# First 21 products of the output projection between the last unit's head pairs, its other operands in the space of queries and keys, the last weight sums in the units

## The chip, the cores and the metric

The kernel runs on one core of one Trainium2 chip. The metric is device microseconds (us) from launch to end. Engines: TensorE (PE, with its weight loads PEld), VectorE (DVE), ScalarE (ACT), GpSimd (POOL), and SyncE (SP), which here issues all DMAs, one after the other: an issue that must wait for a semaphore holds back all issues behind it.

## The reference

All of it is fp32, on x of shape (8, 512, 1024): eight batch elements of 512 rows.

```python
def _L0_attn_ref(h, Wq, Wk, Wv, Wo):            # 16 heads of 64
    q, k, v = h @ Wq, h @ Wk, h @ Wv            # split into heads; rotary embedding on q and k
    logits = where(causal, q @ k.T, -1e9) / sqrt(64)
    return (softmax(logits) @ v) @ Wo

def _L0_ffn_ref(x, weight, bias, lora_A, lora_B, starts):
    y = x @ weight.T + bias
    return y + (x @ A.T) @ Bw.T                 # one of 3 adapters of rank 16 per batch element, or none

x = x + layernorm(attn(layernorm(x), Wq, Wk, Wv, Wo))
x = x + layernorm(ffn(layernorm(x), weight, bias, lora_A, lora_B, starts))
```

## The kernel before

**Products.** Every large matrix product of a batch element (512 x 1024 by 1024 x 1024) is done by the Strassen-Winograd scheme twice over: 7 x 7 = 49 small products instead of 64, at the price of sums of operands and of results. The outer level has seven groups, P1 to P7 (`GROUPS`): P1 is L11·R11, P2 is L12·R21, P4 is L22·T4, P5 is S1·T1, P7 is S3·T3, P6 is S2·T2, P3 is S4·R22, done in that order (`ORDER`). L and S are the weight's blocks and their sums, R and T those of the activations. S1 to S4 and the inner sums of the weights are made once ("weight sums") and kept in DRAM; T1 to T4 are made on the spot by `sum_right`, each from R blocks and the T before: T1 = R12 − R11, T2 = R22 − T1, T4 = R21 − T2, T3 = R22 − R12. Each outer group is seven small products of two matmuls (128x128 weights, 128x256 moving), collected in PSUM accumulators acca to accd, and drained by `drain`: DVE additions into p1 and u2, ACT copies, and results A, U, c11, c12, c21, c22. `combine` adds these to each other on DVE or POOL.

**Ticks.** The order of everything is written out by hand. The list `events` maps a tick, one small product, to the calls that are issued with it (`at(tick, fn)`), and `run(tick, filler)` issues first the events marked "pe", then the product itself, then the rest. All engines and SP take their instructions in that order.

**Stages.**
- The V projection, with the first layer norm, 8 x 49 ticks (until about 432 us).
- Eight units of Q and K projections (`plan_unit`, `unit_product`), 49 ticks each. A unit is a half of the heads for two batch elements. The results (A, B, D, E, F) are added and rotated on DVE and POOL and moved by DMA to the tiles qk. In units 1 to 7 the eight head pairs of the unit before stand between the products (class `Pair`: `scores` s, `exps`, `scale`, `transpose` ptp, `keep` pT, `values` po, `store` ops, `sum` opt). Operands come by DMA through a ring, `load_slot`, eight products ahead.
- The last unit's eight pairs alone ("the tail"), where no unit products are left: `Pair(u, n).plan(base + 51 + 6 * n, alone=True)`. In a pair, scores of the first two query blocks, of the third (s_2) and of the fourth (s_3) come one after another. The fourth block's scores of this unit lie in two of the three accumulator banks `ps_p`, the others in the one buffer `ps_s`. When a batch element's last pair is stored, four POOL sums (`sum`, opt) complete the operand, which SP stores to attn in DRAM. The tile opt has one buffer.
- The output projection of batch elements q = 0 to 7 and the FFN (q = 8 to 15), by `products`, 49 ticks each, with the layer norms, residuals, transposes and the adapters' first product (`lora_in`, ph) of the element before between them.

**Weight sums.** `plan_part` makes one of 24 chunks (8 for the second half of Q and K, 8 for Wo, 8 for the FFN weight): a load of 512 KB, eight sums on POOL, a store of 1568 KB, in one buffer. Units 1 to 7 do three each, the tail does three.

**Memory.** The tail frees the ring and its neighbours (`streams`) and puts the Wo blocks L11, L12, L22, S1 (pool `wop`) and the right operands of q = 0 (pool `gp`) there. S3, S2, S4 (pool `wop2`) and everything that the projection needs otherwise lie in the space of the attention's pools (`phase_a`), so they can only be opened when the attention is through.

**Right operands of the next element.** `plan_right` loads R11, R21, R12, R22 of q + 1 at ticks 10, 17, 24, 31 of q into the tiles that the earlier operands leave (`next_roles`), and makes T1, T2, T4, T3 at 38, 45, 52, 63, on POOL while q + 1 is an output projection.

Of the kernel before, what the change touches and what calls it, by code (L numbers as in the profile page):

```python
# [17 lines left out]
P = 128  # L18
# [114 lines left out]
def sandwich_kernel(  # L133
# [60 lines left out]
    def at(tick, fn, kind=None):  # L194
        events[tick].append((kind, fn) if kind else fn)
# [42 lines left out]

    def load_sums(pool, name, n, tag):

        t = LW[name][n] = pool.tile([P, 8, 7, 64], F32, tag=tag, name=f"{name}_{n}")
        nc.sync.dma_start(out=t, in_=w2_d[name][:, :, 7 * SLOT_L[n] : 7 * SLOT_L[n] + 7])

# [40 lines left out]
    def open_c(q, tag):  # L284
        C[q, tag] = env["cp"].tile(
            [P, 2, HALF], F32, tag=tag, bufs=env["cbufs"] if tag[0] == "c" else 1, name=f"{tag}_{q}"
        )

    class Group:
# [42 lines left out]
        def drain(self, p):  # L332

            acc, t = self.acc, self.t
            add = lambda out, x, a: nc.vector.tensor_tensor(out, acc[a], x, op=ALU.add)  # L335
            if p == "P1":
                for n, k in (("p1", 1), ("u2", 2)):
                    t[n] = env["tmp"].tile([P, SUB], F32, tag=n, bufs=k, name=f"{n}_{self.name}")
# [22 lines left out]

    def products(q0, count, order):


        cur, before, todo = None, None, None

        def fill(q, g, p):
            nonlocal cur, before, todo
            if p == 0:
                before = cur  # L370
                cur = Group(q, order(q)[g]) if q < q0 + count else None
            name = SLOTS[p]
            group = before if name == "P3" else cur
            if group:
                group.product(name)
            if todo:
                todo[0].drain(todo[1])
            todo = (group, name) if group else None

        for n in range(count * N2 + 4):  # L380
            q, m = divmod(n, N2)
            g, p = divmod(m, NP)
            run(n, lambda q=q, g=g, p=p: fill(q0 + q, g, p))
# [26 lines left out]
    def norm(key, dst, src):  # L410
# [8 lines left out]
    env.update(  # L419
        cbufs=1, small=right(stay, "small0", 4), cp=right(stay, "cp0"), tmp=right(stay, "tmp0")  # L420
    )
    gvp, wvp, wvl = (right(operands, name) for name in ("gv", "wv", "wvl"))
    ps_p = env["acc"] = psum.enter_context(tc.tile_pool(name="ps_p0", bufs=1, space=PSUM))
# [169 lines left out]
    PAIRS = B  # L593
    phase_a, streams, work2 = ExitStack(), ExitStack(), {}

# [119 lines left out]
    class Pair:  # L715
# [14 lines left out]
        def scores(self, qbs):  # L730
            qT, kT = (qk[self.u, self.i][:, :, self.s, w] for w in range(2))
            if self.u + 1 == UQ and qbs[0] == 3:
                ps = [
                    ps_p.tile([P, S], F32, tag="acc", name=f"s_{self.name}_{qbs[0]}_{j}") for j in range(2)
                ]
            else:
                ps = ps_s.tile([P, 2, S], F32, tag="s", name=f"s_{self.name}_{qbs[0]}")
                ps = [ps[:, j, :] for j in range(2)]
            at = 0
            for qb in qbs:  # L740
                L = (qb + 1) * P
                for j in range(2):
                    r = slice(j * HD, (j + 1) * HD)
                    nc.tensor.matmul(  # L744
                        ps[j][:, at : at + L],
                        lhsT=qT[r, qb],
                        rhs=kT[r, : qb + 1],
                        start=True,
                        stop=True,
                    )  # L750
                self.ps[qb] = [p[:, at : at + L] for p in ps]
                at += L

        def exps(self, qbs):
            pr = work2["work"].tile([P, 2, S], F32, tag="pr", bufs=4, name=f"pr_{self.name}_{qbs[0]}")
            at = 0
            for qb in qbs:
# [5 lines left out]
                for j in range(2):  # L763

                    nc.vector.tensor_tensor_reduce(  # L765
                        out=v[:, j, :],
                        in0=self.ps[qb][j],
                        in1=work2["mask"][:, S - L :],
# [84 lines left out]
        def plan(self, base, last=12, alone=False):  # L853
# [16 lines left out]
            if self.i == NH - 1:  # L870
                for m, k in enumerate((1, 2, 3, 4, 6)):
                    at(base + last + k, lambda m=m: self.sum(m))
# [67 lines left out]
    cur, before = None, None  # L940

    def unit_product(n):
        nonlocal cur, before
        u, m = divmod(n, N2)
        m, p = divmod(m, NP)
        if p == 0:
            before, cur = cur, quad_group(u, m)
        cur.product(p)
        if p:
            cur.drain(p)  # L950
        elif before:
            before.drain(NP)
        load_slot(n + 8)

    for u in range(UQ + 1):
# [14 lines left out]
        else:  # L970
# [3 lines left out]
            streams.close()  # L974
            wop = tc.alloc_tile_pool(name="w2", bufs=1)
            gp = tc.alloc_tile_pool(name="g2", bufs=1)
            for k, n in ((14, "R11"), (16, "R12"), (18, "R22"), (20, "R21")):
                at(base + k, lambda n=n: load_right(gp, 0, n))
            for k, n in ((24, "L11"), (30, "L12"), (36, "L22"), (42, "S1")):
                at(base + k, lambda n=n: load_sums(wop, "wo", n, n))  # L980
            for k, n in ((26, "T1"), (30, "T2"), (34, "T4"), (38, "T3")):
                for m in range(3):
                    at(base + k + m, lambda n=n, m=m: sum_right(gp, 0, n, nc.gpsimd, slice(m, m + 1)))
            run_rest()
    phase_a.close()


    with ExitStack() as a:
        wop2 = a.enter_context(tc.tile_pool(name="w2b", bufs=1, side="right"))
        cp = a.enter_context(tc.tile_pool(name="cp", bufs=1, side="right"))  # L990
        lc = a.enter_context(tc.tile_pool(name="lc", bufs=1, side="right"))
        rows = a.enter_context(tc.tile_pool(name="rows", bufs=3, side="right"))
# [4 lines left out]
        env.update(acc=ps_p, cp=cp, tmp=tmp, small=small, cbufs=2)  # L997
# [6 lines left out]
        lb_sb = lc.tile([P, E], F32, name="lb_sb")  # L1004
        nc.gpsimd.memset(lb_sb, 0.0)
        env["lb"] = lb_sb
        nc.sync.dma_start(out=lb_sb[0:NR, :], in_=lora_b)
        nc.sync.dma_start(out=lb_sb[HD : HD + NR, :], in_=lora_b)
        nc.sync.dma_start(out=lb_sb[NR : NR + 1, :], in_=bias)

# [158 lines left out]

        load_sums(wop2, "wo", "S3", "S3")  # L1170
        for n, k in (("S2", 3), ("S4", 9)):
            at(k, lambda n=n: load_sums(wop2, "wo", n, n))
        for q in range(NQ):
# [10 lines left out]
            for k, e, res, l, r in (  # L1184
# [7 lines left out]
            ):  # L1192
                at(base + k, lambda a=(q, res, l, r, e): combine(*a))
# [6 lines left out]
    gp.release()  # L1200
    wop.release()

# [90 lines left out]
```

## Time and profile before

| | |
|---|---|
| time, median of 3 runs | 2529.23 us (2528.59 to 2531.31) |
| the profiled execution | 2532.83 us, span 2530.8 us |
| mean granted TensorE clock | 0.984 |
| busy time of PE, DVE, POOL, ACT | 2402.4 (95%), 1733.9 (69%), 1500.0 (59%), 1097.2 us (43%) |
| DMA | 606.00 MB, mean 239 GB/s |
| units 2, 3 and 4 | 148.6 us each |
| the tail | the last unit product is issued at 1578 us; the first product of the output projection starts at 1689.69 us |

The profile is that of one execution. Its page has the busy share of each engine by 40 slices of the span; the trace behind it has each instruction with its start, its time and, in brackets, how long its engine was idle before it and which instruction ended that. Neighbouring instructions of one kind are drawn together (x4 is four of them). Tile names are cut of their numbers: `accb_P<-wo_L,R` is a product of an L block of Wo on an R block; `wo_S` is one of the S blocks.

### The profile page before, as it was taken

The page shows a single profiled execution, that of the slowest core. Times are in us where ns is not written, and L with a number is a line of the kernel's source. Part 1 is how long each engine was busy: PE and PEld are TensorE (multiplying, and loading weights), DVE is VectorE, ACT ScalarE, POOL GpSimd, SP SyncE. Part 2 cuts the span into 40 slices and gives each one's busy share as a digit, 9 for nine tenths or more (in the row PEclk, how much of TensorE's full clock was granted, in tenths as well). Part 3 has the DMA queues.
Part 4 walks back from the last instruction along what each step waited for, and adds up shares of the span by engine and source line. Part 5 has one row for each costly group of instructions (what it writes and reads, how often), then busy time and mean ns, then how long its engine had stood idle before and what let it go on. Part 6 is the DMA issues. An engine that isn't in the chain of part 4 may idle for free. (4 is left out here: it accounts for less than half of the span.)

```text
span 2530.8 us, 37109 instructions
## 1 busy us (share of the span) xinstructions
PE 2402.4 (95%) x12192; PEld 1885.9 (75%) x12192; DVE 1733.9 (69%) x3842; ACT 1097.2 (43%) x2748; POOL 1500.0 (59%) x1127
## 2 busy tenths in 40 slices
PE   6999998989999999999999999788999999999997
PEld 4887887777777777777777766357888887888886
DVE  8777676284957668585775858645777777766676
ACT  3323321025555555555555565752444443222222
POOL 4978774225363453626355363365677686887885
PEclk8999999999999999999999999899999999999999
DMA  7687888899899898989788894766656677334434
GB/s 257 209 281 256 256 262 261 283 292 274 255 311 275 263 317 254 324 250 327 250 272 315 234 316 143 242 230 242 212 167 210 220 266 271 126 130 141 142 104 137
DMA packets 415665, 606.00 MB, mean 239 GB/s; under 512 B 127889, under 2 KB 243601, under 8 KB 410866
## 3 DMA queue, kind: packets, MB, share of 16 engines
q1 hardware_dynamic: 415474, 603.64, 73.2%
q8 instruction: 98, 1.61, 0.3%
q14 instruction: 93, 0.76, 0.1%
HBM read 368.65 MB, written 201.33 MB: 225 GB/s over the span
## 5 line engine op out<-in xcount | busy, mean ns | idle before, releaser
L775 ACT ACTIVATE pr<-pr,nm 128x128 f32<-128x128 f32 (+3 forms) x512 | 280.8, 550 | 173.5 <-DVE nm L765 173.5
L786 ACT ACTIVATE pr<-pr,rs 128x128 f32<-128x128 f32 (+3 forms) x512 | 251.8, 551 | 109.8 <-DVE rs L783 109.8
L765 DVE CUSTOM_DVE_ANT_0 pr<-s,mask 128x128 f32<-128x128 f32 (+3 forms) x512 | 224.2, 484 | 36.6 <-PE s L744 34.6
L632 PE MATMUL accb_q_P<-xs,ls 128*128 128x256 f32 x896 | 218.1, 387 | 6.9 <-DVE u_q_P L116 6.9
L632 PE MATMUL accc_q_P<-xs,ls 128*128 128x256 f32 x896 | 218.6, 387 | 5.4 <-DVE E_q L116 5.4
L632 PE MATMUL acca_q_P<-xs,ls 128*128 128x256 f32 x896 | 219.4, 388 | 0.8 <-issue 0.8
L1040 POOL TENSOR_TENSOR c<-c,row 128x512 f32<-128x512 f32 x120 | 160.6, 1359 | 90.5 <-ACT c L412 84.5
L632 PEld LDWEIGHTS accc_q_P<-xs,ls 128*128 128x128 f32 x896 | 166.3, 191 | 53.4 <-issue 23.7
L632 PEld LDWEIGHTS acca_q_P<-xs,ls 128*128 128x128 f32 x896 | 166.7, 191 | 51.9 <-issue 21.6
L632 PEld LDWEIGHTS accb_q_P<-xs,ls 128*128 128x128 f32 x896 | 166.4, 191 | 51.0 <-DMA ls<-wqk 8.1
L744 PE MATMUL s<-qk 64*128 64x128 f32 (+3 forms) x1024 | 192.9, 471 | 4.2 <-DVE nm L765 2.4
L275 POOL TENSOR_TENSOR T<-R,T 128x512 f32<-128x512 f32 (+1 forms) x96 | 174.0, 1839 | 33.3 <-DVE u_P L335 17.4
L800 PE MATMUL ptp<-ident,pr 128*128 128x128 f32 x1280 | 178.4, 278 | 11.4 <-ACT pr L786 6.7
L800 PEld LDWEIGHTS ptp<-ident,pr 128*128 128x128 f32 x1280 | 147.4, 142 | 46.4 <-ACT pr L786 11.4
L673 POOL TENSOR_TENSOR B_q<-B_q,m 128x1024 f32<-128x1024 f32 x16 | 39.7, 2480 | 237.6 <-DVE B_q L671 237.6
L820 PE MATMUL po<-pT,v 128*64 128x384 f32 (+3 forms) x1024 | 158.8, 448 | 20.8 <-ACT pT L814 17.0
L558 POOL TENSOR_TENSOR wc_g<-wc_g 128x256 f32<-128x256 f32 (+1 forms) x120 | 122.9, 1043 | 90.5 <-DMA wc_g<-in_wqk_dram 74.9
L820 PEld LDWEIGHTS po<-pT,v 128*64 128x64 f32 x1024 | 71.1, 139 | 115.5 <-issue 66.9
L335 DVE TENSOR_TENSOR p_P<-accb_P,p_P 128x256 f32<-128x256 f32 x112 | 46.3, 413 | 107.8 <-PE accb_P L313 58.6
L335 DVE TENSOR_TENSOR u_P<-accb_P,p_P 128x256 f32<-128x256 f32 x112 | 47.3, 423 | 98.1 <-ACT p_P L339 98.1
L814 DVE COPY pT<-ptp 128x512 f32<-128x512 f32 (+1 forms) x136 | 82.8, 614 | 43.5 <-PE ptp L800 43.5
L632 PE MATMUL accd_q_P<-xs,ls 128*128 128x256 f32 x448 | 108.9, 386 | 1.1 <-ACT E_q L125 0.7
(1077 smaller groups left out, 5790.3 us busy)
## 6 DMA issues: line engine op xcount, KB each, us to landing
ls<-wqk SPq DMA_DIRECT2D x392, 256.0 KB, 4.4
xs<-xop SPq DMA_DIRECT2D x392, 256.0 KB, 4.7
R<-attn SPq DMA_DIRECT2D x32, 896.0 KB, 5.5
wqk<-wc_g SPq DMA_DIRECT2D x16, 1568.0 KB, 9.4
x<-in_x_dram SPq DMA_DIRECT2D x32, 512.0 KB, 9.5
v<-vd SPq DMA_DIRECT2D x64, 256.0 KB, 5.2
attn<-ops SPq DMA_DIRECT2D x16, 1024.0 KB, 8.4
row<-in_x_dram SPq DMA_DIRECT2D x32, 512.0 KB, 6.1
```

What stands on the lines that cost most here:

```text
L275: eng.tensor_tensor(RX[q, n][:, c], RX[q, x][:, c], RX[q, y][:, c], op=ALU.subtract)
L335: add = lambda out, x, a: nc.vector.tensor_tensor(out, acc[a], x, op=ALU.add)
L558: eng.tensor_tensor(out, x, y, op=op)
L632: nc.tensor.matmul(acc[:, :, w, :], lhsT=ls[:, k, w, :], rhs=xs_[:, :, k, :], start=(first and w == 0 and k == 0), stop=True, skip_group_c ...
L744: nc.tensor.matmul(ps[j][:, at : at + L], lhsT=qT[r, qb], rhs=kT[r, : qb + 1], start=True, stop=True,)
L765: nc.vector.tensor_tensor_reduce(out=v[:, j, :], in0=self.ps[qb][j], in1=work2["mask"][:, S - L :], scale=-1.0 / HD**0.5, scalar=3.0e38, o ...
L775: nc.scalar.activation(v[:, j, :], v[:, j, :], AF.Exp, bias=nm[:, j : j + 1], scale=-1.0, accum_out=sm[:, j : j + 1],)
L786: nc.scalar.mul(v, v, rs[:, j : j + 1])
L800: nc.tensor.transpose(pt[:, n, :], self.pr[qb][:, j, ts(kb, P)], ident)
L814: copy(self.pT[j][:, : qb + 1, ts(qb, P)], self.pt[j][:, : qb + 1, :])
L820: nc.tensor.matmul(po[j * HD : (j + 1) * HD, kb * P :], lhsT=self.v[:, kb, ts(j, HD)], rhs=self.pT[j][:, kb, kb * P :], start=(kb == 0), s ...
L1040: nc.gpsimd.tensor_tensor(c, c, row[q, t][:, ts(h, HALF)], op=ALU.add)
```

## The change

It has these parts.

- The first 21 products of q = 0 (P1, P2, P4, which need L11, L12, L22, R11, R21, T4) are issued in the tail by a new `first_product`, into accumulators of `ps_p`: eight at ticks 20, 23, … 41, two in each of the periods of pairs 2 to 5, and thirteen at ticks 44 to 56. `products` then begins at tick 21 (`AHEAD`). Accordingly the fourth block's scores go back to the single buffer `ps_s`.
- The tail's pools `wop`, `gp` and two small ones (`cl`, `tl`) are opened after the chunk buffer is closed too; loads of R11 and L11 stand at tick 10, R12 15, R22 17, L12 21, R21 24, L22 31, S1 42; T1 at 21, T2 26, T4 32, T3 44.
- `qk` and its neighbour close at tick 49, before the rest of the attention; S3, S2, S4 are loaded into their space at ticks 49, 54, 56.
- Units 4, 5 and 6 do four chunks of weight sums (ticks 4, 13, 22, 31) instead of three (9, 19, 29), the tail none.
- The opt sums of the last two pairs' elements come at +0, 0, 0, 0, 1 ticks behind their store instead of +1, 2, 3, 4, 6.
- For q = 1, R12, R22, R11, R21 are loaded at ticks 21, 29, 30, 33, T1 at 44; c21 += c12 of q = 0 (tick 38) now stands ahead of T1 on POOL.
- The adapters la_sb and lb_sb are cleared (POOL) and loaded at tick 79 instead of ahead of tick 0.

```diff
-    def load_sums(pool, name, n, tag):
+    def load_sums(pool, name, n, tag, queue=nc.sync):
...
+                env["u2"].reverse()
+                for n, pool in (("p1", env["p1"]), ("u2", env["u2"][0])):
+                    t[n] = pool.tile([P, SUB], F32, tag=n, name=f"{n}_{self.name}")
...
-        for n in range(count * N2 + 4):
+        for n in range(first, count * N2 + 4):
...
-            if self.u + 1 == UQ and qbs[0] == 3:
-                ps = [
-                    ps_p.tile([P, S], F32, tag="acc", name=f"s_{self.name}_{qbs[0]}_{j}") for j in range(2)
-                ]
-            else:
-                ps = ps_s.tile([P, 2, S], F32, tag="s", name=f"s_{self.name}_{qbs[0]}")
-                ps = [ps[:, j, :] for j in range(2)]
+            ps = ps_s.tile([P, 2, S], F32, tag="s", name=f"s_{self.name}_{qbs[0]}")
...
-                for m, k in enumerate((1, 2, 3, 4, 6)):
+                for m, k in enumerate((0, 0, 0, 0, 1) if alone else (1, 2, 3, 4, 6)):
...
-        for name, bufs in (("small", 4), ("ops", 2), ("qk", 5), ("v", 3), ("work", 2), ("ac", 1), ("ch", 1)):
-            work2[name] = right(phase_a, name, bufs)
+        for name, bufs in (("small", 4), ("ops", 2), ("v", 3), ("work", 2), ("ac", 1), ("qk", 5), ("ch", 1)):
+            to = {"ac": rows_qk, "qk": rows_qk, "ch": chunks}.get(name, phase_a)
+            work2[name] = right(to, name, bufs)
...
-        for k in () if u == 0 else (9, 19, 29) if u < UQ else (6, 22, 38):
+        for k in () if u in (0, UQ) else (4, 13, 22, 31) if u in (4, 5, 6) else (9, 19, 29):
...
+    AHEAD = 3 * NP
+
+    def first_product(n):
+        nonlocal cur, before
+        m, p = divmod(n, NP)
+        if p == 0:
+            L, R, tag = GROUPS[ORDER[m]]
+
+            def mm(acc, p, first):
+                l, r, _ = PRODUCTS[p]
+                for k in range(2):
+                    nc.tensor.matmul(
+                        acc, lhsT=RX[0, R][:, SLOT_R[r], k, :],
+                        rhs=LW["wo"][L][:, 4 * k : 4 * k + 4, SLOT_L[l], :],
+                        start=(first and k == 0), stop=True, skip_group_check=True,
+                    )
...
+            before, cur = cur, Product(nc, ps_p, tl, [P, SUB], f"0_{ORDER[m]}", mm, dest)
+        cur.product(p)
+        if p:
+            cur.drain(p)
+        elif before:
+            before.drain(NP)
...
-            wop = tc.alloc_tile_pool(name="w2", bufs=1)
-            gp = tc.alloc_tile_pool(name="g2", bufs=1)
-            for k, n in ((14, "R11"), (16, "R12"), (18, "R22"), (20, "R21")):
-                at(base + k, lambda n=n: load_right(gp, 0, n))
-            for k, n in ((24, "L11"), (30, "L12"), (36, "L22"), (42, "S1")):
-                at(base + k, lambda n=n: load_sums(wop, "wo", n, n))
-            for k, n in ((26, "T1"), (30, "T2"), (34, "T4"), (38, "T3")):
+            chunks.close()
+
+            wop, gp, cl = (tc.alloc_tile_pool(name=name, bufs=1) for name in ("w2", "g2", "cl"))
+            env["cl"] = cl
+            tl = tc.alloc_tile_pool(name="tl", bufs=1)
+            for k, n in (
+                (10, "R11"), (10, "L11"), (15, "R12"), (17, "R22"), (21, "L12"), (24, "R21"), (31, "L22"), (42, "S1"),
+            ):
...
+            for k, n in ((21, "T1"), (26, "T2"), (32, "T4"), (44, "T3")):
                 for m in range(3):
                     at(base + k + m, lambda n=n, m=m: sum_right(gp, 0, n, nc.gpsimd, slice(m, m + 1)))
+            at(base + 52, lambda: combine(0, "c11", "c11", "A", nc.vector))
+            cur, ticks = None, [*range(20, 44, 3), *range(44, 57)]
+            for k in range(10, 57):
+                if k in (54, 56):
+                    n = {54: "S2", 56: "S4"}[k]
+                    load_sums(wop2, "wo", n, n)
+                if k == 49:
+                    rows_qk.close()
+                    wop2 = tc.alloc_tile_pool(name="w2b", bufs=1)
+                    load_sums(wop2, "wo", "S3", "S3")
+                if k in ticks:
+                    run(base + k, lambda n=ticks.index(k): first_product(n))
+                else:
+                    run(base + k, None)
+            cur.drain(NP)
...
-        nc.gpsimd.memset(la_sb, 0.0)
-        nc.sync.dma_start(out=la_sb[:, :, 0:NR], in_=lora_a.rearrange("(k p) r -> p k r", p=P))
...
+        def load_adapters():
+            nc.gpsimd.memset(la_sb, 0.0)
...
+        at(N2 + 30, load_adapters)
...
-            at(base + 6, next_roles)
+            at(max(base + 6, AHEAD), next_roles)
             for n, k in (("R11", 10), ("R21", 17), ("R12", 24), ("R22", 31)):
+                if q == 1:
+                    k = AHEAD + {"R12": 0, "R22": 8, "R11": 9, "R21": 12}[n]
...
-            for n, k in (("T1", 38), ("T2", 45), ("T4", 52), ("T3", 63)):
+            for n, k in (("T1", 44 if q == 1 else 38), ("T2", 45), ("T4", 52), ("T3", 63)):
...
-        load_sums(wop2, "wo", "S3", "S3")
-        for n, k in (("S2", 3), ("S4", 9)):
-            at(k, lambda n=n: load_sums(wop2, "wo", n, n))
...
-        products(0, NQ, lambda q: ORDER if q + 1 < NQ else LAST)
+        products(0, NQ, lambda q: ORDER if q + 1 < NQ else LAST, AHEAD)
```

More of the change, by code (lines that the diff above doesn't have):

```diff
@@ L237, in sum_left @@
         eng.tensor_tensor(W[n][:, c], W[x][:, c], W[y][:, c], op=op)
-    def load_sums(pool, name, n, tag):
+    def load_sums(pool, name, n, tag, queue=nc.sync):
         t = LW[name][n] = pool.tile([P, 8, 7, 64], F32, tag=tag, name=f"{name}_{n}")
-        nc.sync.dma_start(out=t, in_=w2_d[name][:, :, 7 * SLOT_L[n] : 7 * SLOT_L[n] + 7])
+        queue.dma_start(out=t, in_=w2_d[name][:, :, 7 * SLOT_L[n] : 7 * SLOT_L[n] + 7])
     def open_right(pool, q, n):
@@ L284, in open_c @@
     def open_c(q, tag):
-        C[q, tag] = env["cp"].tile(
-            [P, 2, HALF], F32, tag=tag, bufs=env["cbufs"] if tag[0] == "c" else 1, name=f"{tag}_{q}"
+        first = q >= 0 and (tag == "A" or tag in ("c11", "c21") and q % 2 == 0)
+        two = q >= 0 and tag in ("c12", "c22")
+        C[q, tag] = env["cl" if first else "cp"].tile(
+            [P, 2, HALF], F32, tag=tag, bufs=1 + two, name=f"{tag}_{q}"
         )
@@ L336, in drain @@
             if p == "P1":
-                for n, k in (("p1", 1), ("u2", 2)):
-                    t[n] = env["tmp"].tile([P, SUB], F32, tag=n, bufs=k, name=f"{n}_{self.name}")
+                env["u2"].reverse()
+                for n, pool in (("p1", env["p1"]), ("u2", env["u2"][0])):
+                    t[n] = pool.tile([P, SUB], F32, tag=n, name=f"{n}_{self.name}")
                 nc.scalar.copy(t["p1"], acc["a"])
@@ L360, in sandwich_kernel, with products @@
     )
-    def products(q0, count, order):
+    def products(q0, count, order, first=0):
         cur, before, todo = None, None, None
@@ L419, in sandwich_kernel @@
     env.update(
-        cbufs=1, small=right(stay, "small0", 4), cp=right(stay, "cp0"), tmp=right(stay, "tmp0")
+        small=right(stay, "small0", 4), cp=right(stay, "cp0"), p1=right(stay, "tmp0")
     )
+    env["u2"] = [env["p1"], right(stay, "tmp1")]
     gvp, wvp, wvl = (right(operands, name) for name in ("gv", "wv", "wvl"))
@@ L593, in sandwich_kernel @@
     PAIRS = B
-    phase_a, streams, work2 = ExitStack(), ExitStack(), {}
+    phase_a, chunks, rows_qk, streams, work2 = *(ExitStack() for _ in range(4)), {}
     def start_ring():
@@ L744, in scores @@
                     nc.tensor.matmul(
-                        ps[j][:, at : at + L],
+                        ps[:, j, at : at + L],
                         lhsT=qT[r, qb],
@@ L750, in scores @@
                     )
-                self.ps[qb] = [p[:, at : at + L] for p in ps]
+                self.ps[qb] = ps[:, :, at : at + L]
                 at += L
@@ L766, in exps @@
                         out=v[:, j, :],
-                        in0=self.ps[qb][j],
+                        in0=self.ps[qb][:, j, :],
                         in1=work2["mask"][:, S - L :],
@@ L939, in sandwich_kernel @@
     assert not todo
-    cur, before = None, None
+    cur = before = tl = None
     def unit_product(n):
@@ L953, in unit_product, with dest @@
         load_slot(n + 8)
+    AHEAD = 3 * NP
[12 more added lines that the diff above has]
+                    )
+            def dest(i, j):
+                if (0, tag) not in C:
+                    open_c(0, tag)
+                return C[0, tag][:, j, ts(i, SUB)]
+            before, cur = cur, Product(nc, ps_p, tl, [P, SUB], f"0_{ORDER[m]}", mm, dest)
[4 more added lines that the diff above has]
+            before.drain(NP)
     for u in range(UQ + 1):
@@ L974, in sandwich_kernel @@
             streams.close()
-            wop = tc.alloc_tile_pool(name="w2", bufs=1)
-            gp = tc.alloc_tile_pool(name="g2", bufs=1)
-            for k, n in ((14, "R11"), (16, "R12"), (18, "R22"), (20, "R21")):
-                at(base + k, lambda n=n: load_right(gp, 0, n))
-            for k, n in ((24, "L11"), (30, "L12"), (36, "L22"), (42, "S1")):
-                at(base + k, lambda n=n: load_sums(wop, "wo", n, n))
-            for k, n in ((26, "T1"), (30, "T2"), (34, "T4"), (38, "T3")):
+            chunks.close()
[5 more added lines that the diff above has]
+            ):
+                if n in ("R11", "R12", "R21", "R22"):
+                    at(base + k, lambda n=n: load_right(gp, 0, n))
+                else:
+                    at(base + k, lambda n=n: load_sums(wop, "wo", n, n))
+            for k, n in ((21, "T1"), (26, "T2"), (32, "T4"), (44, "T3")):
                 for m in range(3):
                     at(base + k + m, lambda n=n, m=m: sum_right(gp, 0, n, nc.gpsimd, slice(m, m + 1)))
+            at(base + 52, lambda: combine(0, "c11", "c11", "A", nc.vector))
[10 more added lines that the diff above has]
+                    run(base + k, lambda n=ticks.index(k): first_product(n))
+                else:
+                    run(base + k, None)
+            cur.drain(NP)
             run_rest()
@@ L988, in sandwich_kernel @@
     with ExitStack() as a:
-        wop2 = a.enter_context(tc.tile_pool(name="w2b", bufs=1, side="right"))
+        rows = a.enter_context(tc.tile_pool(name="rows", bufs=3, side="right"))
+        lc = a.enter_context(tc.tile_pool(name="lc", bufs=1, side="right"))
         cp = a.enter_context(tc.tile_pool(name="cp", bufs=1, side="right"))
-        lc = a.enter_context(tc.tile_pool(name="lc", bufs=1, side="right"))
-        rows = a.enter_context(tc.tile_pool(name="rows", bufs=3, side="right"))
         small = a.enter_context(tc.tile_pool(name="small2", bufs=3, side="right"))
@@ L996, in sandwich_kernel @@
         ps_t = a.enter_context(tc.tile_pool(name="ps_t2", bufs=2, space=PSUM))
-        env.update(acc=ps_p, cp=cp, tmp=tmp, small=small, cbufs=2)
+        env.update(acc=ps_p, cp=cp, p1=tl, u2=[tl, tmp], small=small)
         la_sb = lc.tile([P, NK, HD], F32, name="la_sb")
-        nc.gpsimd.memset(la_sb, 0.0)
-        nc.sync.dma_start(out=la_sb[:, :, 0:NR], in_=lora_a.rearrange("(k p) r -> p k r", p=P))
[L1004 to L1009, printed above, removed]
+        lb_sb = env["lb"] = lc.tile([P, E], F32, name="lb_sb")
+        def load_adapters():
+            nc.gpsimd.memset(la_sb, 0.0)
+            nc.sync.dma_start(out=la_sb[:, :, 0:NR], in_=lora_a.rearrange("(k p) r -> p k r", p=P))
+            nc.gpsimd.memset(lb_sb, 0.0)
+            nc.sync.dma_start(out=lb_sb[0:NR, :], in_=lora_b)
+            nc.sync.dma_start(out=lb_sb[HD : HD + NR, :], in_=lora_b)
+            nc.sync.dma_start(out=lb_sb[NR : NR + 1, :], in_=bias)
+        at(N2 + 30, load_adapters)
         NQ = 2 * B
@@ L1192, in sandwich_kernel @@
             ):
-                at(base + k, lambda a=(q, res, l, r, e): combine(*a))
+                if base + k >= AHEAD:
+                    at(base + k, lambda a=(q, res, l, r, e): combine(*a))
             if q + 1 < NQ:
@@ L1197, in sandwich_kernel @@
                 plan_last(q, base)
-        products(0, NQ, lambda q: ORDER if q + 1 < NQ else LAST)
+        products(0, NQ, lambda q: ORDER if q + 1 < NQ else LAST, AHEAD)
         run_rest()
-    gp.release()
-    wop.release()
+    for pool in (wop2, tl, cl, gp, wop):
+        pool.release()
 _OUTS = [((B, S, E), "float32")]
```

## The prediction

> **What bounds the kernel now.** I read the busy slices first (40 equal slices, a digit for tenths of busy time or of the clock), then PE's timeline where it dips, POOL's behind that, and windows by unit.
>
> ```profile
> PE   6999998989999999999999999788999999999997
> ...
> PEclk8999999999999999999999999899999999999999
> ```
>
> TensorE (PE) is busy nearly throughout; after the start its one dip stands at slices 26 to 28 (1582 to 1771 us), where a granted clock of 0.8 shows too: the last unit's pairs alone, then the first output projections. PE's timeline there, in pieces (start, busy time, engine, line, operation; in brackets the idle time before it and what ended it):
>
> ```profile
> 1636.93 2.37 PE L820 MATMUL po<-pT,v 128*64 128x512 f32 x16 [1.90 <-ACT pT L814]
> 1639.23 0.88 PE L800 MATMUL ptp<-ident,pr 128*128 128x128 f32 x6
> 1640.04 0.92 PE L744 MATMUL s<-qk 64*128 64x384 f32 x4
> ...
> 1643.29 1.09 PE L800 MATMUL ptp<-ident,pr 128*128 128x128 f32 x8 [0.47 <-DVE pT L814]
> 1644.31 0.93 PE L744 MATMUL s<-qk 64*128 64x128 f32 x8
> 1647.14 1.08 PE L820 MATMUL po<-pT,v 128*64 128x512 f32 x4 [1.90 <-ACT pT L814]
> ```
>
> A pair alone takes 1647.14 − 1636.93 = 10.2 us with 1.90 + 0.47 us of PE idle; ScalarE (ACT) is busy 18.28 of 20 us (1640 to 1660). The period is a ring through ACT's pT copy, po, ptp, the scores and ACT's exponentials. The end of the tail, from ptp of pair 6 at 1669.83 on:
>
> ```profile
> 1677.70 4.54 PE L820 MATMUL po<-pT,v 128*64 128x512 f32 x16 [2.76 <-ACT pT L814]
> ...
> 1686.82 2.94 PE L820 MATMUL po<-pT,v 128*64 128x512 f32 x16 [0.21 <-ACT pT L814]
> 1689.69 1.13 PE L313 MATMUL accb_P<-wo_L,R 128*128 128x256 f32 x4
> ```
>
> In these 20 us PE waits 4.18 us, and po takes 4.54 instead of 2.37 us: the clock fell to 0.65 (1675 to 1680). Products then follow one per 0.865 us.
>
> Then two waits and a late sum:
>
> ```profile
> 1716.29 1.10 PE L313 MATMUL accb_P<-wo_S,R 128*128 128x256 f32 x4 [3.02 <-issue]
> ...
> 1744.85 1.65 PE L313 MATMUL accb_P<-wo_L,R 128*128 128x256 f32 x3 [4.19 <-DVE u_P L335]
> ...
> 1755.08 1.13 PE L313 MATMUL accb_P<-wo_L,T 128*128 128x256 f32 x4 [0.56 <-POOL T L275]
> ```
>
> The first is S3 (landed 1716.09), loaded only after the attention closes. In the second VectorE (DVE) stands behind c21 on GpSimd (POOL), which stands behind T1:
>
> ```profile
> 1733.57 6.14 POOL L275 TENSOR_TENSOR T<-R,R 128x512 f32<-128x512 f32 x3 [31.27 <-DMA R<-attn]
> 1739.68 2.48 POOL L352 TENSOR_TENSOR c<-c,c 128x512 f32<-128x512 f32 x2
> 1742.12 6.22 POOL L275 TENSOR_TENSOR T<-R,T 128x512 f32<-128x512 f32 x3
> ...
> 1750.75 4.27 POOL L275 TENSOR_TENSOR T<-R,T 128x512 f32<-128x512 f32 x3
> ```
>
> My checkpoint C is 1755.08, projection 1's first product on T4 (tick 63). Behind it both kernels run the same stages, so the gain at C is the gain at the end, less what comes later.
>
> **The products between the pairs.** Eight stand in pairs 2 to 5. Four lie between a ptp and the next pair's scores, on the ring: 4 × 0.865 = 3.46 us; two ACT copies of an accumulator (0.37 us each, by the pT copy of 256 elements) lie on it too, 0.74. The other four follow the last scores, in the 1.90 us idle, and cost nothing; without that cover 3.46 more. So ptp of pair 6 moves from 1669.83 to 1674.0 (bounds 1672 and 1677.5). Scores going back to one buffer wait for DVE's reads of the scores before; DVE takes them up later than that anyway and idles 3.64 us per period, so I put it at nothing, 0.4 us per pair if uncovered. First R11 and L11 must be there. R11's tile is issued after the last qk moves (landed 1618.21), so about 1618.3; the spacings of such loads back to back (2.2 us for R, 4.7 for a weight sum, after some 2 us) put L11 at 1627. Its product stands behind the ptp at 1629.94: no wait, with 2 to 3 us to spare.
>
> **The other thirteen.** From 1669.83 to 1689.69 PE spends 19.86 us: 4.18 idle, 3.57 of low clock (2.17 in po of pair 6, 0.57 in the last po, 0.83 in two ptp), so 12.1 of work. With 13 × 0.865 = 11.25 among it PE is nearly full, the clock holds, and tick 21 is reached at 1674.0 + 12.1 + 11.25 = 1697.4; up to 3 us later if po still waits on ACT. Before, tick 21 stood at 1689.69 + 21 × 0.865 = 1707.9: 10.5 us gained of 18.2 moved.
>
> **Operands in the space of queries and keys.** S3 can be issued when pair 7's scores have been read, about 1682, lands about 1688.5 and is needed at 1703: the 3.02 us go, with 1.25 us of low clock behind them. c21 now stands ahead of T1 on POOL, so 4.19 us and 1.6 us of low clock go (the clock stood at 0.68 from 1745 to 1750). Forty-two ticks at 0.865 bring PE to T4's place at 1697.4 + 36.3 = 1734.
>
> **What is late next: T4.** The copy of pair 6's output now stands on DVE behind the drain of a product, at about 1690 (1684.2 before). Three more sums on POOL (1.27 us each) end at 1694.3; their store must land (6.3 us, the longer store before) before the next sums overwrite the tile, at 1701; four sums to 1706.3. Only then does SyncE (SP), which issues everything in order, issue pair 7's stores, and R12, R22, R11, R21 of projection 1 stand behind them. The transfers queue up: S4 to 1709.9, stores + 4.4, four R at 2.2 each, so R11 lands at 1720.9 and R21 at 1723.1. T1 5.2 (rows 4.27 and 6.14), T2 6.2, c21 2.5, T4 4.5: 18.4 us from 1721, so T4 is ready at 1739.4, against PE at 1734: a wait of 5.4 us, bounds 0.5 (all T sums at 4.3 and earlier loads) and 8.5. R11's own margin (needed at 1721.6) is under 1 us, but a wait there shortens the one for T4.
>
> [...]
>
> C is therefore at 1739.4 instead of 1755.08: 15.7 us. The wait lowers the clock as the one of 4.19 us did: minus 1.6 (bounds 0 and 2.5). [...]
>
> **Adapters.** Their two clears and four loads, 7.5 us to landing, move to tick 79, on POOL behind a row's addition (ends 1769.55, C + 14.5). The loads land at C + 22.6; ph needs them at C + 21.5: minus 1.1 us (bounds 0 and 2.5).
>
> **Weight sums.** The three chunks of the tail (8 sums each, 7.5 us, off PE's path) cost nothing there. Units 4 to 6 get a fourth each. PE has no idle time in units 2 to 6 (148.60 of 148.60 us), POOL 71 of 148.6 us, the transfers a share of 0.87, so only lateness can cost. The fourth chunk's load waits for the third's store (8.2 us), and six of its sums stand on POOL ahead of F's addition, which today ends at 1078.15 in unit 4 and is wanted by DVE at 1079.62: 1.5 us of slack, and I work the addition out to 1079.5. I take 0.5 us in all, bounds 0 and 3.
>
> **Sum.** 15.7 − 1.6 − 1.1 − 0.5 = 12.5 us against the profiled execution (2532.83 us, span 2530.8). That run is 3.6 us above the median of 2529.23; I subtract from the median: 2516.7.
>
> **Rivals.**
> - T4 is not late: if POOL sums at 4.3 us and the loads get through 2 us earlier, PE is never stopped and C falls at 1734: 21 − 1.1 − 0.5 = 19.4 us, 2510. For it: 4.27 us at 1750.75; against it: the neighbours at 6.14 and 6.22.
> - The early products stall the pairs: if L11 or R11 land late, or all eight products lie on ACT's ring (7.66 us instead of 4.2) and thirteen do not fill the waits, tick 21 comes 5 us later, and R's chain with it: 7 us gained, 2522. For it: ACT has under 2 us of 20 free, and a load took 8.66 us at 1624. Against it: the 2 us margin.
> - Slower: the fourth chunk. If F's addition slips past its 1.5 us, DVE's rotation waits, and behind it on DVE the drains of PE's accumulators, so PE stops in three units. A whole chunk (7.5 us) exposed three times costs 22.5: 2539. It decides from (12.5 + 5) / 3, about 6 us per unit. For it: only 1.5 us of slack, and SP held about 2 us at the load with ring loads behind it. Against it: the ring runs eight products (24 us) ahead.
> - The products only move: if they lengthen the tail one for one (18.2 us) and R's chain slips with it, only 3.02 + 4.19 and their clock (10 us in all) go, less T4's wait and the small terms, 8.6: 2528, no change. Against it: 4.18 us of idle and 3.57 of low clock in the last 20 us alone.
>
> **How the numbers follow.** Forecast 0.50, no T4 wait 0.17, stalled pairs 0.15, no change 0.08, slower 0.10. Faster by over 0.2% (5 us, about what a measurement can tell from no change) is the first three: 0.82; same 0.08; slower 0.10. The range runs from the second case, 2509, past the third to 2524, and leaves out the last two: 0.18.
>
> **What would show it.** Right: pair periods near 11.2 us; the last po ending near 1696 at a full clock; no 3.02 and no 4.19; a wait of 2 to 8 us of accb on wo_L,T with POOL T as releaser near 1739; T1 starting when R11 lands at about 1721; a wait of about 1 us at ph; units 4 to 6 still at 148.6 us. Wrong: idle PE in units 4 to 6, a first product waiting on a transfer, T4 on time, or pair periods of 12 us.

## The result and the profile after

The changed kernel takes 2518.04 us (median of 5 runs, 2516.67 to 2518.93), the kernel before 2529.23 us in the same comparison: 11.2 us less, a ratio of 0.9952 with a 95% interval of 0.9938 to 0.9967. A second measurement of the same two, on another occasion, gave 2521.33 us (12 runs, 2515.57 to 2528.06) against 2529.06: 0.9971, interval 0.9960 to 0.9982. The forecast was 2516.7 us, in a range of 2509 to 2524.

The profiled execution took 2516.67 us (span 2514.9), 16.2 us less than the profiled one of before. 1.5 us of that were there before any line of the change ran (the first unit starts at 430.6 instead of 432.1 us, and the last one at 1412.2 instead of 1413.7). So I compare traces by the time from the last unit's first product to checkpoint C, projection 1's first product on T4: 1755.08 − 1413.7 = 341.4 us before, 1739.03 − 1412.2 = 326.8 us after. **The trace's gain at the change is 14.6 us.** Behind C nothing more is gained or lost: `ph` of the first rows comes 16.0 us earlier, and the span ends 15.9 us earlier.

The busy slices of the changed kernel (tenths of busy time and of the granted clock) have a dip that is one slice shorter: slice 28 has 9 instead of 8. The clock's row is what it was, with its 0.8 in slice 26, in the first pairs alone, which have no products:

```profile
PE   6999999989999999999999999789999999999997
...
PEclk8999999999999999999999999899999999999999
```

PE's timeline in the changed kernel, one pair alone (start, busy time, engine, line, operation, and in brackets the idle time before it with what ended it):

```profile
1636.87 2.37 PE L818 MATMUL po<-pT,v 128*64 128x512 f32 x16 [1.35 <-ACT pT L812]
1639.17 0.87 PE L798 MATMUL ptp<-ident,pr 128*128 128x128 f32 x6
1639.88 1.03 PE L965 MATMUL accc_P<-wo_L,R 128*128 128x256 f32 x4
1640.84 0.92 PE L742 MATMUL s<-qk 64*128 64x384 f32 x4
...
1642.90 1.13 PE L742 MATMUL s<-qk 64*128 64x512 f32 x4 [0.34 <-DVE nm L763]
1643.96 1.13 PE L965 MATMUL accb_P<-wo_L,R 128*128 128x256 f32 x4
...
1647.91 2.37 PE L818 MATMUL po<-pT,v 128*64 128x512 f32 x16 [1.09 <-ACT pT L812]
```

The period is 11.04 us instead of 10.2, with two products in it; line 965 is `first_product`. The 0.34 us are the price of the single score buffer (the fourth scores wait until VectorE has read the third). They fall into time that the pair has to wait anyway: in products_after_pairs below, which has the single buffer and no products in the pairs, four periods take 40.76 us, as in the kernel before.

The end of the tail and the first product of `products` (line 315):

```profile
1682.39 2.37 PE L818 MATMUL po<-pT,v 128*64 128x512 f32 x16
...
1692.93 2.38 PE L818 MATMUL po<-pT,v 128*64 128x512 f32 x16
1695.23 1.13 PE L965 MATMUL accc_P<-wo_L,T 128*128 128x256 f32 x4
1696.93 1.10 PE L315 MATMUL accb_P<-wo_S,T 128*128 128x256 f32 x4 [0.56 <-issue]
```

The two po take 2.37 and 2.38 us, at a full clock (1.00 from 1680 to 1695) and without a wait; before, they took 4.54 and 2.94, with 2.76 us of idle time ahead of the first. Tick 21 is reached at 1696.93. Then the waits that took the place of 3.02 and 4.19 us:

```profile
1722.73 1.79 PE L315 MATMUL accb_P<-wo_L,R 128*128 128x256 f32 x4 [2.25 <-DMA R<-attn]
1735.59 1.13 PE L315 MATMUL accb_P<-wo_L,R 128*128 128x256 f32 x4 [0.55 <-DVE u_P L337]
1739.03 1.13 PE L315 MATMUL accb_P<-wo_L,T 128*128 128x256 f32 x4 [1.44 <-POOL T L275]
```

POOL's timeline says why:

```profile
1722.84 4.25 POOL L275 TENSOR_TENSOR T<-R,R 128x512 f32<-128x512 f32 x3 [10.06 <-DMA R<-attn]
1727.05 5.25 POOL L275 TENSOR_TENSOR T<-R,T 128x512 f32<-128x512 f32 x3
1732.27 2.48 POOL L355 TENSOR_TENSOR c<-c,U 128x512 f32<-128x512 f32 x2
1734.72 4.26 POOL L275 TENSOR_TENSOR T<-R,T 128x512 f32<-128x512 f32 x3
```

T1 starts as soon as R11 has landed, and T1, T2, c21 and T4 run without a gap until T4 lets PE go on. From tick 21 to C are 42.1 us, of which 36.3 are products; the three waits are 4.24, and the clock behind the first wait (0.81 from 1720 to 1725, 0.85 from 1725 to 1730) costs 5 × 0.19 + 5 × 0.15 = 1.7.

### The profile page after: what moved, and what is told of

The parts are those of the page before. It is cut to its first block, busy times and chain, and to the rows that moved or that the text cites. A ratio compares the mean times of both kernels' runs of the same rounds, so it can differ in the third digit from the quotient of the medians.

```text
span 2514.9 us, 37116 instructions
## 1 busy us (share of the span) xinstructions
PE 2399.3 (95%) x12192; PEld 1882.0 (75%) x12192; DVE 1745.5 (69%) x3842; ACT 1096.5 (44%) x2748; POOL 1508.8 (60%) x1127
```

## The experiments

Each kernel was compared with the kernel before in its own comparison (median of before 2528.12 us in the first four, 2529.98 in the next three, 2529.06 in the last two). "To C" is the time from the last unit's first product to checkpoint C in the kernel's profile. "C to ph" is the time from there to the adapters' first product. The medians scatter by some microseconds, so the traces carry the verdicts. Three profiles with the same tail and the same projections (changed, chunk_at_34, changed_again) agree on 326.8 us to C; the other kernels have one profile each.

| kernel | median, us | ratio, 95% interval | to C | tick 21 to C | C to ph |
|---|---|---|---|---|---|
| before | 2529.23 | | 341.4 | 47.2 | 21.5 |
| changed | 2518.04 | 0.9938 to 0.9967 | 326.8 | 42.1 | 21.5 |
| products_after_pairs | 2520.72 | 0.9961 to 0.9982 | 330.0 | 36.1 | 22.3 |
| s_late | 2532.61 | 1.0005 to 1.0030 | 341.5 | 56.6 | 25.7 |
| r_early | 2518.13 | 0.9952 to 0.9977 | 323.6 | 39.5 | 21.5 |
| c21_behind_t1 | 2520.74 | 0.9968 to 0.9987 | 330.2 | 45.7 | 21.5 |
| sums_alone | 2530.55 | 0.9993 to 1.0015 | 339.6 | 45.4 | 21.0 |
| chunk_at_34 | 2516.03 | 0.9935 to 0.9959 | 326.8 | 42.1 | 21.5 |
| r_and_c21_early | 2515.01 | 0.9923 to 0.9950 | 322.5 | 39.0 | 23.2 |
| c21_on_vector | 2513.82 | 0.9923 to 0.9952 | 322.5 | 39.8 | 21.6 |
| changed_again | 2521.33 | 0.9960 to 0.9982 | 326.8 | 42.1 | 27.2 |

The earlier opt sums and the moved adapters have no run of their own.

**products_after_pairs.** The products go behind the last pair.

```diff
-            at(base + 52, lambda: combine(0, "c11", "c11", "A", nc.vector))
...
-                if k in ticks:
-                    run(base + k, lambda n=ticks.index(k): first_product(n))
-                else:
-                    run(base + k, None)
+                run(base + k, None)
+            run_rest()
+            for n in range(AHEAD):
+                first_product(n)
+                if n == 16:
+                    combine(0, "c11", "c11", "A", nc.vector)
             cur.drain(NP)
-            run_rest()
```

> The changed kernel, with its 21 early products issued after the last pair instead of between the pairs (all loads and sums stay where the change put them). My theory: the tail's pairs go as in the kernel before, tick 21 comes about 9.5 us later, but R12, R22, R11, R21 are then no longer late, so the waits for R11 (2.25 us) and T4 (1.44) and their low clock (1.7) go: checkpoint C about 4 us later than in the changed kernel, time about 2522. Rival A (the products between the pairs are the whole of the gain): 2528 to 2529. Rival B (the gain is all in S3 and c21, the products only moved): 2518.

The tail looks like that of before again (PE's timeline, the last two po):

```profile
1674.44 3.74 PE L818 MATMUL po<-pT,v 128*64 128x512 f32 x16 [2.75 <-ACT pT L812]
...
1682.22 2.94 PE L818 MATMUL po<-pT,v 128*64 128x512 f32 x16 [0.21 <-ACT pT L812]
```

Measured from the second pair's po (1623.51 here, 1625.55 in the changed kernel), tick 21 comes 80.5 us later here and 71.4 there: 18.2 us of products cost 9.0 us between the pairs and gain 9.2. The eight cost 44.72 − 40.76 = 4.0 us over four periods, the thirteen the other 5.0. But the waits for R11 and T4 are gone here, and C is only 3.2 us later than in the changed kernel. My theory held; of 9.2 us earned between the pairs, 6.0 are given back at the loads and sums of projection 1. Rival A asked for 10 us more and falls, and so does rival B in the trace, though the medians alone (2520.72 against 2518.04 and 2521.33) would not say so.

**s_late.** S3, S2, S4 are loaded behind the last pair's stores.

```diff
-                if k in (54, 56):
-                    n = {54: "S2", 56: "S4"}[k]
-                    load_sums(wop2, "wo", n, n)
...
             run_rest()
+            for n in ("S3", "S2", "S4"):
+                load_sums(wop2, "wo", n, n)
```

> The changed kernel, with S3, S2, S4 loaded after the last pair's stores instead of at ticks 49, 54, 56. My theory: the parts are not additive; with the products earlier, S3 (landing about 1716) is needed at 1703, so PE waits about 13 us, the four R loads slip behind, and C comes about 9.5 us later: 2527 to 2528, nearly the whole gain lost. Rival (additive: only the wait of 3.02 us and its low clock of 1.25 come back): 2522.

```profile
1718.22 2.04 PE L315 MATMUL accb_P<-wo_S,R 128*128 128x256 f32 x4 [15.02 <-DMA wo_S<-wo_d]
```

The wait of 3.02 us grew to 15.02 us, and C lies where it lay before the change (341.5 against 341.4). It is 14.7 us later than in the changed kernel, where I expected 9.5: besides the 15.02 us PE waits 2.55 us for a drain at 1750.96, and the products behind both are slow (2.04 us at 1718.22 and 1.91 at 1751.94, where the changed kernel's take 1.03 at a full clock). The kernel is slower than before by a little, but clear of noise; in its profile 4.2 us are lost between C and `ph`, some 2 to slow products (2.08 us at 1754.40 instead of 1.13, 1.91 at 1756.26 instead of 1.03), the rest to a wait of 2.34 us, with an addition of VectorE ahead of it that takes 4.19 us, 1.92 in the changed kernel:

```profile
1760.35 4.19 DVE L355 TENSOR_TENSOR c<-c,A 128x1024 f32<-128x1024 f32 x1
```

(changed_again below has it longer still.) The parts do not add: without S3 in the space of queries and keys, the 21 products gain nothing, since they only bring PE sooner to a weight that is not there.

**c21_behind_t1.** T1 of projection 1 goes back ahead of c21.

```diff
-            for n, k in (("T1", 44 if q == 1 else 38), ("T2", 45), ("T4", 52), ("T3", 63)):
+            for n, k in (("T1", 38), ("T2", 45), ("T4", 52), ("T3", 63)):
```

> The changed kernel, with T1 of projection 1 put back to tick 38, so ahead of c21 on POOL. My theory: c21 then waits for R11 too, VectorE stands behind it until about 1729.6, PE stops for about 4 us on a drain, T4 comes 2.5 us later: C 2.6 to 4.5 us later, 2520.6 to 2522.5. Rival (R11's wait covers it already): no change, 2518.

PE's timeline has the drain's wait back, beside those for R11 (2.40) and T4 (1.43):

```profile
1735.25 1.13 PE L315 MATMUL accb_P<-wo_L,R 128*128 128x256 f32 x4 [3.22 <-DVE u_P L337]
```

VectorE's timeline has what it stood behind:

```profile
1732.60 2.27 DVE L355 TENSOR_TENSOR c<-c,c 128x1024 f32<-128x1024 f32 x1 [8.59 <-POOL c L355]
```

To C it is 3.4 us more than in the changed kernel, as I expected. VectorE is free at 1732.60, or 1729.5 without the 3.1 us by which this profile's last unit starts later (expected 1729.6), and PE stops for 3.22 us (expected 4). c21's place ahead of T1 is a part of the gain by itself; the medians alone (2520.74 against 2518.04 and 2521.33) would not say so.

**r_early.** R12, R11 and R21 are issued ahead of the last pair's stores.

```diff
             cur.drain(NP)
+            next_roles()
+            for n in ("R12", "R11", "R21"):
+                load_right(gp, 1, n)
             run_rest()
...
-            at(max(base + 6, AHEAD), next_roles)
+            if q > 1:
+                at(base + 6, next_roles)
...
-                    k = AHEAD + {"R12": 0, "R22": 8, "R11": 9, "R21": 12}[n]
+                    if n != "R22":
+                        continue
+                    k = AHEAD + 8
```

> The changed kernel, with R12, R11, R21 of projection 1 issued before the last pair's stores instead of behind them (R22 stays at tick 29). My theory: the R chain behind those stores is what is late now; T1 starts near 1712 instead of 1722.8, the waits of 2.25, 0.55 and 1.44 us go and the low clock (1.7 us) with them: about 5.9 us less, 2512. Rival (POOL's sums, not the loads, make T4 late): the wait on T4 stays at 1 us or more, and no more than 3 us are gained, 2515. A third, that the loads ahead only push back the stores and S4: no gain, 2518.

No wait for R11 is left, but PE's wait for VectorE, which stands behind c21, grew (PE, then POOL, then VectorE):

```profile
1735.22 1.33 PE L315 MATMUL accb_P<-wo_L,R 128*128 128x256 f32 x4 [2.21 <-DVE u_P L337]
```

```profile
1718.51 6.30 POOL L275 TENSOR_TENSOR T<-R,R 128x512 f32<-128x512 f32 x3 [3.54 <-PE acca_P L315]
1727.19 4.74 POOL L275 TENSOR_TENSOR T<-R,T 128x512 f32<-128x512 f32 x3 [2.39 <-DMA R<-attn]
```

```profile
1733.19 0.69 DVE L395 BATCH_NORM_STATS2 bn_o<-c 128x6 f32<-128x512 f32 x1 [3.50 <-POOL c L355]
```

C comes 3.2 us earlier, not 5.9; that is near the rival's 3, but not by its sign, since the wait for T4 is 0.39 us. Counted from tick 21, T1 starts 6.5 us earlier (R11 landed at 1718.35), but it takes 6.30 instead of 4.25 us, and T2 waits for R22, behind the stores. c21's second sum stands behind T2, VectorE behind c21, PE behind VectorE. The profiled execution is only 0.7 us shorter than the changed kernel's, since units 4 to 6 took 449.7 us in it, 2.6 more than there. The median shows none of the gain either; whether for the same reason, no run shows. That leads to the weight sums.

**sums_alone** and **chunk_at_34.** The first is the kernel before with only the chunks moved; the second the changed kernel with the fourth chunk three ticks later.

```diff
-        for k in () if u == 0 else (9, 19, 29) if u < UQ else (6, 22, 38):
+        for k in () if u in (0, UQ) else (4, 13, 22, 31) if u in (4, 5, 6) else (9, 19, 29):
```

```diff
-        for k in () if u in (0, UQ) else (4, 13, 22, 31) if u in (4, 5, 6) else (9, 19, 29):
+        for k in () if u in (0, UQ) else (4, 13, 22, 34) if u in (4, 5, 6) else (9, 19, 29):
```

> The kernel before, with only the weight sums moved (four chunks in units 4 to 6, at ticks 4, 13, 22, 31; none in the tail). My theory: nothing gained in the tail (POOL's work there is off PE's path), and in units 4 to 6 between 0 and 3 us per unit lost, in some executions, where F's addition stands behind six sums of a late chunk and VectorE's rotation waits for it: 0 to 4 us slower in all, 2528 to 2532. Rival (the chunks' transfers and sums hold up the tail): 2 to 3 us faster, 2525.

> The changed kernel, with the fourth chunk of units 4 to 6 loaded at tick 34 instead of 31, so that its sums stand behind F's addition on POOL. My theory: VectorE's wait on F goes, units 4 to 6 take 148.6 us each in every profile, and the time falls by 0 to 3 us against the changed kernel, 2515 to 2518. Rival (the units' lateness comes from the transfers of the chunk, not from POOL's order): units still up to 151 us.

In the profile of r_early, unit 5 takes 151.4 us. POOL's timeline there, and VectorE's waits (in all, times, longest):

```profile
1222.72 5.34 POOL L562 TENSOR_TENSOR wc_wf<-wc_wf 128x256 f32<-128x256 f32 x6 [10.45 <-DMA wc_wf<-in_wf_dram]
1228.02 4.67 POOL L654 TENSOR_TENSOR F_q<-F_q,E_q 128x1024 f32<-128x1024 f32 x2
```

```profile
DVE m L672 <- POOL F_q L654: 1.9, 1, 1.9
```

Six sums wait for the chunk's load, F's addition waits for the six, VectorE's rotation for F, and PE for 1.9 us in that unit. This is the mechanism of the prediction's slower rival, with 2.6 us in three units instead of 22.5. (c21_behind_t1 has it too, 449.5 us in the three units; changed_again, the same code there, 445.9.) With the load at tick 34, POOL's order is turned round:

```profile
1220.75 4.69 POOL L654 TENSOR_TENSOR F_q<-F_q,E_q 128x1024 f32<-128x1024 f32 x2 [10.90 <-DVE F_q L116]
1225.39 9.56 POOL L562 TENSOR_TENSOR wc_wf<-wc_wf 128x256 f32<-128x256 f32 x8
```

VectorE's wait on F is gone in this profile, as my theory has it. Units 4 to 6 still took 447.0 us, two of them 149.2; so that part of the expectation failed, though the kernel before has 447.0 as well; the rival's 151 did not come either. The moved sums alone neither gain nor lose: 1.0004, interval 0.9993 to 1.0015. (In their profile C is 1.8 us nearer than in that of before: S3's wait is 2.21 us instead of 3.02, and the products behind it take 1.03 us, where those of before ran at a clock of 0.50 from 1717.5 to 1720.8. One profile can't tell this from scatter.)

**r_and_c21_early** and **c21_on_vector.** Besides the chunk at tick 34, R22 takes the tile that R21 leaves, so that it can be loaded ahead of the stores, and T2 stands behind c21's second sum; in the second kernel that sum is VectorE's.

```diff
+            next_roles()
+            role["R21"], role["R22"] = role["R22"], role["R21"]
+            for n in ("R12", "R11", "R22"):
+                load_right(gp, 1, n)
             run_rest()
...
-            for n, k in (("T1", 44 if q == 1 else 38), ("T2", 45), ("T4", 52), ("T3", 63)):
+            for n, k in (("T1", 44 if q == 1 else 38), ("T2", 48 if q == 1 else 45), ("T4", 52), ("T3", 63)):
```

```diff
-                (46, dve, "c22", "c22", "U"), (47, pool, "c21", "c21", "U"),
+                (46, dve, "c22", "c22", "U"), (47, pool if q else dve, "c21", "c21", "U"),
```

> The changed kernel with the fourth chunk at tick 34, with R12, R11, R22 of projection 1 issued before the last pair's stores (R22 in the tile that R21 leaves, R21 at tick 29 in T1's), and T2 of projection 1 put behind the sum c21 += U on POOL. My theory: VectorE no longer stands behind c21, T2 no longer waits for R22; from tick 21 to checkpoint C 36.5 to 37.5 us instead of 42.1, about 5 us less, and 1 to 2 us less in the units: 2511 to 2513. Rival (the transfers from 1697 to 1727 are the bound, whatever their order): 39.5 us from tick 21 to C, as with R12, R11, R21 early alone, 2515 to 2516.

> The kernel of r_and_c21_early with the sum c21 += U of element 0 on VectorE (one addition, 1.7 to 2.2 us) instead of GpSimd. My theory: GpSimd's sums T1, T2, T4 and c21, slowed by VectorE's additions beside them, are what is late now; without c21's 4.47 us T4 is ready about 4 us earlier, the wait of 3.12 us and its low clock go, and tick 21 to checkpoint C takes 36.5 to 37.5 us instead of 38.95: 2513. Rival (VectorE's extra 2 us delay the drains, and PE waits for those): 39 us or more, 2515 or more.

In the first, the waits for R11 and for VectorE are gone and one for T4 is left:

```profile
1735.27 2.08 PE L315 MATMUL accb_P<-wo_L,T 128*128 128x256 f32 x4 [3.12 <-POOL T L275]
```

```profile
1716.11 6.24 POOL L275 TENSOR_TENSOR T<-R,R 128x512 f32<-128x512 f32 x3 [3.93 <-DMA R<-attn]
1722.30 4.47 POOL L355 TENSOR_TENSOR c<-c,U 128x512 f32<-128x512 f32 x2
1726.73 8.48 POOL L275 TENSOR_TENSOR T<-R,T 128x512 f32<-128x512 f32 x6
```

Counted from tick 21, T1 starts 6.1 us earlier than in the changed kernel, but the same eleven POOL instructions take 19.1 us instead of 16.1: T1 (6.24 instead of 4.25) and c21 (4.47 instead of 2.48) now lie beside VectorE's own additions. Neither my 36.5 to 37.5 us nor the rival's 39.5 was met exactly, but 39.0 is the rival's side. With c21 on VectorE, T4 is in time, but VectorE needs 4.92 us for two sums beside T1 and PE waits 2.35 us for a drain; C does not move (322.5). Its rival was right in the trace, though the median is nearer my 2513 than its 2515. Both kernels beat the changed one in the trace by 4.3 us to C; the first loses 1.7 of them again before `ph`, as the two products behind its wait for T4, at C and behind it, take 2.08 and 1.55 us instead of 1.13 and 1.03. Their medians, 2515.01 and 2513.82, are the lowest of all; the better of the two can't be told from these runs.

**changed_again.** The changed kernel a second time.

> The changed kernel itself, unchanged, on the chip of this comparison: 2518, tick 21 to checkpoint C 42 us, with the same three waits of 2.25, 0.55 and 1.44 us; units 4 to 6 between 446 and 450 us in all.

The three waits came back to 0.01 us and 42.1 us to C. But this profiled execution, 2521.34 us, has one wait more, behind C: PE's line, then VectorE's and POOL's beside it.

```profile
1749.16 2.08 PE L315 MATMUL acca_P<-wo_S,T 128*128 128x256 f32 x4 [4.46 <-ACT c L349]
```

```profile
1741.55 6.12 DVE L355 TENSOR_TENSOR c<-c,A 128x1024 f32<-128x1024 f32 x1
```

```profile
1739.87 4.28 POOL L275 TENSOR_TENSOR R<-R,R 128x512 f32<-128x512 f32 x3
1744.09 2.50 POOL L1091 TENSOR_TENSOR c<-c,row 128x512 f32<-128x512 f32 x2
```

In the first profile the same addition took 1.92 us and POOL's T3 (R<-R,R) 5.27:

```profile
1743.05 1.92 DVE L355 TENSOR_TENSOR c<-c,A 128x1024 f32<-128x1024 f32 x1
```

```profile
1741.39 5.27 POOL L275 TENSOR_TENSOR R<-R,R 128x512 f32<-128x512 f32 x3
```

Here it lasted until POOL's five instructions were over, and everything behind it on VectorE came late: from C to `ph` 27.2 us instead of 21.5. That is 5.7 us; the two profiled executions (2521.34 and 2516.67) are 4.7 us apart.

## Why the prediction was right

**Right in mechanism and near in size.** The trace's gain is 14.6 us for 12.5 forecast, the medians' 11.2 and 7.7. At C the forecast was 15.7 us and 14.6 were found; the 1.6 and 1.1 us that it took off behind C were not lost there. (Times of the changed profile stand 1.5 us early against the forecast's, which go by the profile of before.)

- The ring of the pairs: forecast 4.2 us for eight products, found 4.0, with periods of 11.0 to 11.3 us for 11.2. The cover named for the four free ones (the idle time ahead of po) is what shrank, from 1.90 us to between 0.9 and 1.4. R11 and L11 were in time: L11 landed at 1627.58, the product started at 1628.57; the margin of 2 to 3 us was 1.
- The end of the tail: tick 21 was put at 1697.4 and came at 1696.93, or 1698.4 without those 1.5 us. The thirteen products needed 0.32 and 0.56 us of waits that the sum had left out.
- S3 was issued at 1680.22 and landed at 1688.44 (forecast 1682 and 1688.5), and its wait is gone. c21's is 0.55 instead of nothing.
- T4: the sum put it at 1739.4, and it came at 1739.03, or 1740.5 without those 1.5 us, by errors that largely cancel. R11 landed at 1722.7, not 1720.9. The loads waited in SP's queue for the stores as predicted (stores issued at 1706.43, forecast 1706.3, the first R at 1707.99), but S4, ahead of all these transfers, landed at 1711.71, not 1709.9, and the rest followed it in the spacings of the forecast. And the POOL sums took 16.1 us, not 18.4: T1 (4.25) came after VectorE's three additions, and T2 (5.25) beside one of them. So the wait is split, 2.25 us at R11 and 1.44 at T4, 4.24 with c21's, for 5.4 in one piece; the sign that the prediction named, 2 to 8 us on T4 itself, was not met.
- The low clock: 1.6 forecast, 1.7 found, though behind the wait of 2.25 us for R11, and so ahead of C instead of behind it.

**The term that was mis-sized.** The adapters were charged 1.1 us and cost nothing: la_sb took 5.0 us to land, not 7.5, and landed at 1758.99, 1.5 us ahead of `ph`. Why it was quicker is not shown: the core moved 283 GB/s while it was under way, 311 before. That and the 0.5 us for the units (447.1 us in units 4 to 6 after, 447.0 before) are 1.6 of the 2.1 us that the trace has gained over the forecast. (The prediction read 148.60 us for every unit; the profile of before already has 149.67 in unit 5.)

**What the prediction did not have.** It subtracted a difference of two profiles from a median, so that 2518.04 came within 1.4 us of 2516.7 is in part luck: the second measurement came out 4.6 above it. One addition's luck (1.92 or 6.12 us) moves what follows by 5.7 us, more than all the small terms together (3.2). Whether it is this that spreads the changed kernel's times from 2515.57 to 2528.06 us is open: only profiled executions show it.

**The rivals.** That T4 would not be late did not come. The stalled pairs did not either. The slower rival's place was right, its size was not: PE was stopped for at most 2.1 us in one unit (c21_behind_t1, unit 5, of 151.6 us), not 7.5 in each of three. That the products only move has something in it: had S3 stayed where it was, they would have (s_late).

## What to carry to other kernels

Work moved into an idle engine's gaps is worth what the next thing needed after it can take: here 9.2 us earned between the pairs became 3.2 at the next operand. So price a move at the first point where a load or a sum of another engine decides, and move that load too; the parts of such a change are not additive. Where an instruction stands in a queue matters more than when it could run: c21 behind T1 (3.22 us in c21_behind_t1), six sums ahead of F (1.9 us in r_early) and loads behind a store (2.25 us in the changed kernel) each stopped PE, through two other engines, with nothing slow in them.

## What the hardware showed

**VectorE beside GpSimd.** In the changed kernel's output projections, an addition of 128x1024 on VectorE takes 1.22 to 1.23 us where no GpSimd instruction overlaps it, and 1.30 to 2.18 beside GpSimd; 4.19 (s_late) and 6.12 (changed_again) were seen once each. Three GpSimd sums take 4.25 us with VectorE idle (changed kernel, 1722.84) and up to 6.30 beside VectorE (r_early). In changed_again VectorE's addition began within a run of five GpSimd instructions (1739.87 to 1746.59), which took 4.28 and 2.50 us, as without it, and ended at 1747.67, 1.1 us after the last of them, about what it takes undisturbed: by this it had got nothing in between. Why, no run shows.

**The clock falls behind some short waits.** A wait of 2.25 us was followed by mean clocks of 0.81 and 0.85 over two stretches of 5 us, as 2.76 us were by 0.65 in the kernel before. Looked at more closely, the clock is 0.50 from 1723.1 to 1726.4 and 1.00 on either side, which is where the 1.7 us come from; the product at 1724.31, at 0.50, takes 1.91 us, those at 1.00 take 1.03. The length of the wait does not decide alone: behind 2.21 us in r_early the product at 1736.35 takes 1.91 us, behind 2.21 us in sums_alone (1717.05) and 3.22 us in c21_behind_t1 (1736.22) it takes 1.03. In the traces of the kernel before and the changed one, up to 2490 us, the stretches of half clock last 3.41 us or a multiple and start a multiple of 3.41 us apart (in the changed kernel at 1583.1, 1596.8 and 1723.1). Between 1580 and 2490 us, in these two traces, PE had been idle for at least 2.0 us of the 3.41 us ahead of each stretch, and for at most 1.6 us of the 3.41 us ahead of each step of this length at the full clock. (Earlier a few came after less, such as 1.05 us at 1451.2 before and 1.20 us at 1450.0 after.) Whether the place of a wait on these steps decides, no run was made to test.

**Queued transfers.** With S2, S4, two stores and four R loads issued within some 16 us (1694.8 to 1711.1), an R load of 896 KB took 10.3 to 14.5 us to land, against 4.6 alone (issued at 1733.39), while the core moved about 400 GB/s (399 from 1700 to 1720 us). Changing their order moved the waits, not the end of the last one: it landed 28.0 us after tick 21 in the changed kernel, and T2, which waited for it, started 28.1 us after tick 21 with three of the four issued early (r_early, 1727.19).
